# A graph network's issue order: seeds for a greedy planner, one per short stretch, in place of a small search

## The chip, the cores and the metric

The kernel runs on one core of one Trainium2 chip. The core has five engines that work side by side, each through its own queue and in order: PE (matrix multiply; PEld is its weight load, which overlaps the multiplies), DVE (vector), ACT (activation functions), POOL (general, slower than DVE) and SP, which here only issues DMA transfers. The metric is the time on the device in microseconds, from first to last instruction, and lower is better.

## The reference, cut to what matters

The input x holds 64 graphs of 256 nodes with 128 features, and one adjacency matrix of 256 x 256 serves all of them. Four layers follow one another, each closed by x = layernorm(x + layer(x)):

```python
for _ in range(5):                                     # layer 0: a gated recurrent graph network
    m = adj @ h
    u3 = h @ u3_w.T + u3_b
    z = sigmoid([m, m] @ w3_w.T + w3_b + u3)
    r = sigmoid([m, m] @ w4_w.T + w4_b + u3)
    hv = tanh([m, m] @ w5_w.T + w5_b + (r * h) @ u5_w.T + u5_b)
    h = (1 - z) * h + z * hv
y1 = (A * I) @ (x @ W[0]) + (A * (1 - I)) @ (x @ W[1]) + bias   # layer 1, A a softmax over edges
g  = relu(layernorm((softmax(scores) * adj) @ (x @ Wp + bp)))   # layer 2: attention, then an MLP
y2 = relu(relu(layernorm(((1 + eps) * g + adj @ g) @ W1 + b1)) @ W2 + b2 + g)
y3 = x @ V0 + sum_k (adj^k @ x) @ Vk                   # layer 3: powers 1 to 3, two sets of weights
```

Everything is in 32-bit floats. The graphs don't depend on one another.

## The kernel before, in words

The graphs are taken in 32 pairs. A tile of 128 partitions by 512 elements holds a pair: two graphs, two halves of the nodes, 128 features. One pair passes through the layers in a long chain of dependent steps, so many pairs are in flight together, and the order in which their steps stand in each engine's queue decides how well the engines are filled.

**The list of operations.** The code first records every step, without issuing it: `Schedule.add` takes the ways in which a step can be done (an engine, an expected duration in us, a function that issues it), what it reads and what it writes. `pe`, `act`, `dve`, `pool`, `evacuate`, `sum_` and `load` are short forms of it. Several steps have two or three ways, such as a sum by DVE or by POOL, or a copy out of PSUM by ACT or by DVE. A name "DVE+" is a DVE operation that uses the SBUF port which POOL uses too, so the planner lets it and a POOL operation exclude each other (`USES`, "PORT").

**The planner.** `order` places the operations one at a time. Of those whose predecessors are placed it takes the one with the smallest key (planned start, due time, number). The planned start is the latest of: its predecessors' ends with the latency to be seen and a lag of 0.3 us, a free buffer of each class it needs, and the free engine. Durations outside PE are multiplied by 1.1 (`MARGIN`). The due time (`op.late`) is 15 us per pair (12 for the last twelve), less the length of the rest of the pair's chain, with an offset for its layer. The result is one list, and the engines' queues are filled in its order. Buffers are given out by the planner too: 15 tiles for x (class X), 4 for the transposed input (T), 8 PSUM banks (PS), and so on.

**The search in it.** `run` goes ahead for 60 us of planned time (`WINDOW`) from a state (`Track`). From each state that was kept, 8 continuations are tried (`TRIES`). The first has no seed, the others add to the due time a pseudo-random number of up to 2 us (`NUDGE`), which depends on the operation's number and the seed. `place` keeps a second clock beside the planned one, with durations without margin and short latencies (`SOON`). It gives a "real" idle time of PE. The 4 states with the least idle time by both clocks (`KEPT`, `IDLE`) go on to the next window.

**The steps that the change touches.**
- `load_x` and `load_h` (by way of `load`, L348) bring a pair's input from DRAM, 256 KB each. The planner's three DMA numbers are the wait before the transfer, the transfer, and the time until its end is seen.
- `spread` (L636 on) multiplies adj with a pair: four matmuls of 256 columns. `spread7` (L647 on) does the same with seven matmuls of 128 columns and six sums on DVE or POOL, and one more copy out of PSUM. `FIRST` says from which pair on layer 0 uses `spread7`; before it, `spread` followed by `to_sbuf`.
- `scale_stats` and `scale_tokens` normalise (sums of squares, then a scaling), by ACT, DVE or POOL. `polynomial7` computes layer 3 with four sums of 256 columns.
- `turn` transposes a tile by a DVE transpose of 32x32 blocks, a write to DRAM and four reads back (L623, L625, L631). Every such DMA, every load and every store stands in SP's queue.

Of the kernel before, what the change touches and what calls it, by code (L numbers as in the profile page):

```python
# [24 lines left out]
FIRST, FINAL = 2, 0  # L25
# [33 lines left out]
SOON = {"PE": 0.2, "ACT": 0.17, "DVE": 0.15, "POOL": 0.15, "SP": 0.0}  # L59

WINDOW, TRIES, KEPT, NUDGE, IDLE = 60.0, 8, 4, 2.0, 0.3
# [45 lines left out]
class Schedule:  # L107
# [29 lines left out]
    def prepare(self, tiles):  # L137

        for op in self.ops:
            for b in op.before:  # L140
                b.then.append(op)
        for op in reversed(self.ops):
            us = min(w[1] for w in op.ways) + op.seen
            op.rest = us + max((x.rest for x in op.then if x.pair == op.pair), default=0.0)
        values = {}
        for op in self.ops:
            op.base = op.ways[0][0].rstrip("+-")
            op.late = self.due(op.pair) - op.rest + HOLD[op.layer] if op.pair >= 0 else -1e4
            op.plans = [(w[0], w[1] * (1.0 if w[0] == "PE" else MARGIN), w[1], USES.get(w[0], (w[0],)), SPARE.get(w[0], 0.0), k)
                        for k, w in enumerate(op.ways)]  # L150
            op.slots = []
            for v in op.holds:
                if v.cls:
                    if v not in values:
                        v.left, values[v] = 0, len(values)
                    v.left += 1
                    op.slots.append((values[v], v.cls, v.seeded, v.full or v.seeded))
        self.values = list(values)
        t = Track()
        t.waits = [len(op.before) for op in self.ops]  # L160
        t.since = [0.0] * len(self.ops)
        t.left, t.until, t.home = [v.left for v in values], [0.0] * len(values), [None] * len(values)
        t.free = {cls: [(0.0, k) for k in range(len(ts))] for cls, ts in tiles.items()}
        t.full = frozenset()
        t.engines, t.real = (dict.fromkeys([*SEEN, "PORT"], 0.0) for _ in range(2))
        t.ready, t.trail, t.number = [op for op in self.ops if not op.before], None, 0
        t.moved = t.real_moved = t.idle = t.real_idle = t.end = 0.0
        t.ends, t.owner, t.released = [0.0] * len(self.ops), {}, {}
        return t

    def run(self, t, until, seed):

        ready, engines, real = t.ready, t.engines, t.real
        while ready:
            best, homes = None, {}
            for op in ready:
                held = t.since[op.number]
                for v, cls, seeded, _ in op.slots:
                    if t.home[v] is None:
                        h = homes.get((cls, seeded))  # L180
                        if h is None:
                            h = homes[cls, seeded] = min((s for s, k in t.free[cls] if not seeded or (cls, k) in t.full),
                                                         default=1e9)
                        held = max(held, h)
                if held == 1e9:
                    continue
                way = None
                for engine, us, _, uses, spare, k in op.plans:
                    start = held
                    for e in uses:  # L190
                        start = max(start, engines[e])
                    if way is None or start + us + spare < way[0]:
                        way = start + us + spare, start, k
                late = op.late
                if seed and op.pair >= 0:
                    late += NUDGE * ((op.number * 7919 + seed * 104729) * 2654435761 % 4294967296 / 2147483648.0 - 1.0)
                key = (way[1], late, op.number)
                if best is None or key < best[0]:
                    best = key, op, way[2]
            if best is None:  # L200
                t.idle = t.real_idle = 1e9
                return
            (start, _, _), op, k = best
            if start >= until:
                return
            self.place(t, op, k, start)

    def place(self, t, op, k, start):

        engine, us, real_us, uses, _, _ = op.plans[k]  # L210
        base, engines, real = engine.rstrip("+-"), t.engines, t.real
        t.ready.remove(op)
        began = max(real[e] for e in uses)
        idle = began
        for x in op.before:
            later = 0.0 if x.base == base == "PE" else 0.05 if x.base == base != "SP" else SOON[x.base]
            began = max(began, t.ends[x.number] + later)
        for v, cls, seeded, full in op.slots:
            if t.home[v] is None:
                slot = min((s for s in t.free[cls] if not seeded or (cls, s[1]) in t.full), key=lambda s: s[0])  # L220
                t.free[cls].remove(slot)
                t.home[v] = slot[1]
                t.owner[v] = t.released.get((cls, slot[1]), 0.0)
            began = max(began, t.owner[v])
        if base == "PE":
            t.idle += start - engines["PE"]
            t.real_idle += began - idle
        end, real_end = start + us, began + real_us
        for e in uses:
            engines[e], real[e] = end, real_end  # L230
        seen, done = SEEN[base] + LAG, real_end + SOON[base]
        if op.dma:
            wait, move, after = op.dma
            t.moved = max(t.moved, end + wait) + move * MARGIN
            t.real_moved = max(t.real_moved, real_end + wait) + move
            seen, done = t.moved + after - end + LAG, t.real_moved + after
        t.ends[op.number] = done - SOON[base]
        t.end = max(t.end, done)
        t.trail, t.number = (t.trail, start, op, k), t.number + 1
        for v, cls, seeded, full in op.slots:  # L240
            home = cls, t.home[v]
            t.released[home] = max(t.released.get(home, 0.0), done)
            t.left[v] -= 1
            t.until[v] = max(t.until[v], end + seen)
            if not t.left[v]:
                t.free[cls].append((t.until[v], t.home[v]))
                t.full = t.full | {home} if full else t.full - {home}
        for x in op.then:
            t.waits[x.number] -= 1
            same = engine != "SP" and x.base == base  # L250
            t.since[x.number] = max(t.since[x.number], end + (AGAIN.get(base, 0.0) if same else seen))
            if not t.waits[x.number]:
                t.ready.append(x)

    def order(self, tiles):

        tracks, until, seed = [self.prepare(tiles)], 0.0, 0
        while any(t.ready for t in tracks):
            until += WINDOW
            found = []  # L260
            for t in tracks:
                for k in range(TRIES if t.ready else 1):
                    c = t.copy()
                    seed += 1
                    self.run(c, until, seed * bool(k))
                    found.append(c)
            tracks = sorted(found, key=lambda t: t.real_idle + IDLE * t.idle)[:KEPT]
        best = min((t for t in tracks if t.number == len(self.ops)), key=lambda t: t.end)
        self.span, self.best = max(best.engines.values()), best
        for v, k in zip(self.values, best.home):  # L270
            v.ap = tiles[v.cls][k]
        out, trail = [], best.trail
        while trail:
            trail, start, op, k = trail
            out.append((start, op.number, op, op.ways[k][2]))
        return [(op, fn) for _, _, op, fn in sorted(out, key=lambda x: x[:2])]


class Track:


    def copy(self):
        c = Track()
        for k, v in self.__dict__.items():
            setattr(c, k, dict(v) if type(v) is dict else list(v) if type(v) is list else v)
        c.free = {cls: list(s) for cls, s in self.free.items()}
        return c
# [3 lines left out]
def kernel(ctx: ExitStack, tc: tile.TileContext, x, xT, adj, adjT, mats, cols, rows, out):  # L291
# [65 lines left out]
    def load_h(p):  # L357
        load(lambda: hTs[p].at(2, N), xT[2 * p:2 * p + 2].rearrange("b d n -> d b n"), hTs[p])
# [720 lines left out]
```

## Time and profile before

| | |
|---|---|
| time, median of 3 runs | 1486.96 us (1486.75 to 1487.11) |
| profiled execution | 1486.49 us, span 1484.7 us |
| PE busy | 1468.3 us (99%) |
| DVE busy | 1270.5 us (86%) |
| ACT busy | 1044.6 us (70%) |
| POOL busy | 899.5 us (61%) |
| DMA | 216.65 MB, queue q1 at 71.4% of 16 engines |
| mean granted PE clock | 0.998 |

The span runs from the first to the last instruction. Busy time is the time in which an engine had an instruction running; the ends of matmuls are modelled, so a PE that is busy throughout isn't one at its peak. In lines of the profile, "L660 PE MATMUL ps<-aT,x" is line 660, on PE, writing a PSUM tile (ps) from the tiles aT and x. One matmul in 32-bit floats stands as two records. "[2.47 <-DMA x<-x_in]" means that the engine stood idle for 2.47 us ahead of this and that the load of x from its input was what it waited for. A view cut into stretches gives the busy time of each engine in each, with the clock that PE was granted (1.00 is full) and the busy share of the DMA engines.

### The profile page before, as it was taken

The numbers are of one execution on the slowest core, as the hardware profiler recorded it, in microseconds if no ns is written. First come the engines' busy times: TensorE is split into PE (matmuls) and PEld (weight loads), VectorE is DVE, ScalarE is ACT, GpSimd is POOL, SyncE is SP. The second block draws the span as 40 slices with busy tenths as digits, with TensorE's granted clock in tenths as the row PEclk, the third lists the DMA queues.
The fourth block names the chain that finished last, engine by engine and source line by source line (L and its number), as shares of the span: only waits on it lengthen the run. The fifth ranks groups of instructions, "written<-read, shape, count | busy, mean of one in ns | idle before, by whom it ended". The sixth has DMA issues, their size and how long they took to land.

```text
span 1484.7 us, 28833 instructions
## 1 busy us (share of the span) xinstructions
PE 1468.3 (99%) x8064; PEld 1066.6 (72%) x8064; DVE 1270.5 (86%) x3182; ACT 1044.6 (70%) x3185; POOL 899.5 (61%) x1383
## 2 busy tenths in 40 slices
PE   9999999999999999999999999999999999999997
PEld 6556666666677677777677777777777776788986
DVE  7867978989899899988889888888988879899973
ACT  4444566667788777776778786777777668789875
POOL 4322445465677687767755666556766656679752
PEclk9999999999999999999999999999999999999999
DMA  8544556778788887788787687767888766768662
GB/s 239 121 86 102 107 119 122 149 154 151 151 167 164 169 172 146 160 165 169 143 156 148 148 163 154 149 149 138 161 164 165 151 146 115 144 146 147 136 129 71
DMA packets 946848, 216.65 MB, mean 146 GB/s; under 512 B 726016, under 2 KB 942208, under 8 KB 946688
## 3 DMA queue, kind: packets, MB, share of 16 engines
q1 hardware_dynamic: 946688, 214.81, 71.4%
q8 instruction: 65, 1.06, 0.3%
q14 instruction: 95, 0.78, 0.2%
HBM read 116.86 MB, written 97.85 MB: 145 GB/s over the span
## 4 chain that ended last, share of the span: by engine, by line
PE 92%; DVE 5%; DMA 1%; ACT 1%; issue 1%; SPq 0%; POOL 0%; POOLq 0%; ACTq 0%; DVEq 0%
PE ps L660 23%; PE ps L778 9%; PE ps L779 9%; PE ps L786 9%; PE ps L793 9%; PE ps L794 9%; PE ps L815 7%; PE ps L994 5%; PE ps L915 4%; PE ps L1017 3%; PE ps L642 2%; PE ps L875 2%; DMA x<-x_in 1%; DVE a L623 0%; DVE x L711 0%
## 5 line engine op out<-in xcount | busy, mean ns | idle before, releaser
L660 PEld LDWEIGHTS ps<-aT,a 128*128 128x128 f32 x2144 | 290.2, 192 | 76.7 <-issue 66.5
L324 ACT COPY a<-ps 128x512 f32<-128x512 f32 (+2 forms) x588 | 243.0, 433 | 112.7 <-PE ps L660 41.3
L660 PE MATMUL ps<-aT,a 128*128 128x128 f32 x2144 | 315.8, 275 | 0.6 <-POOL a L666 0.6
L797 ACT ACTIVATE ps<-ps,bzrh 128x512 f32<-128x512 f32 x160 | 105.8, 661 | 108.7 <-PE ps L794 107.1
L782 ACT ACTIVATE a<-ps,bzrh 128x512 f32<-128x512 f32 x160 | 110.1, 688 | 102.1 <-PE ps L779 99.6
L739 ACT ACTIVATE a<-ps 128x128 f32<-128x128 f32 x496 | 130.9, 285 | 53.6 <-PE ps L815 20.4
L779 PE MATMUL ps<-a,w 128*128 128x512 f32 x320 | 164.3, 595 | 0.0
L793 PE MATMUL ps<-a,w 128*128 128x512 f32 x320 | 163.7, 593 | 0.5 <-DVE a L761 0.5
L679 POOL TENSOR_TENSOR a<-a 128x128 f32<-128x128 f32 x202 | 101.8, 508 | 103.0 <-DVE a L675 91.8
L794 PE MATMUL ps<-a,u5h 128*128 128x512 f32 x320 | 163.4, 592 | 0.0
L786 PE MATMUL ps<-a,w 128*128 128x512 f32 x320 | 163.4, 594 | 0.0
L623 DVE STREAM_TRANSPOSE a<-a 128x512 f32<-128x512 f32 x215 | 149.6, 698 | 2.4 <-ACT ps L324 0.4
L681 DVE TENSOR_TENSOR a<-ps,a 128x256 f32<-128x256 f32 x234 | 96.3, 415 | 60.0 <-ACT a L324 32.5
L815 PEld LDWEIGHTS ps<-W,a 128*128 128x128 f32 x1024 | 131.4, 192 | 15.7 <-issue 13.6
L815 PE MATMUL ps<-W,a 128*128 128x128 f32 x1024 | 142.7, 275 | 0.0
L747 POOL TENSOR_TENSOR s<-s,neg_half 128x4 f32<-128x4 f32 x128 | 138.2, 1080 | 6.9
L788 ACT ACTIVATE a<-ps,bzrh 128x512 f32<-128x512 f32 x160 | 110.6, 691 | 42.8 <-PE ps L786 39.0
L675 POOL TENSOR_TENSOR a<-a 128x256 f32<-128x256 f32 x114 | 84.9, 746 | 88.2 <-ACT a L324 85.9
L778 PE MATMUL ps<-a,W 128*128 128x512 f32 x256 | 131.6, 596 | 0.0
L779 PEld LDWEIGHTS ps<-a,w 128*128 128x128 f32 x320 | 61.1, 191 | 77.0 <-issue 68.2
L799 DVE SCALAR_TENSOR_TENSOR ps<-a,ps 128x512 f32<-128x512 f32 x160 | 109.3, 683 | 7.9 <-ACT a L788 6.4
L794 PEld LDWEIGHTS ps<-a,u5h 128*128 128x128 f32 x320 | 60.8, 190 | 76.5 <-issue 64.3
(229 smaller groups left out, 3454.9 us busy)
## 6 DMA issues: line engine op xcount, KB each, us to landing
e<-a SPq DMA_DIRECT2D x277, 256.0 KB
a<-e SPq DMA_DIRECT2D x1108, 64.0 KB
e<-b SPq DMA_DIRECT2D x32, 512.0 KB
b<-e SPq DMA_DIRECT2D x128, 128.0 KB
x<-x_in SPq DMA_DIRECT2D x32, 256.0 KB
t<-xT_in SPq DMA_DIRECT2D x32, 256.0 KB
a<-d SPq DMA_DIRECT2D x32, 256.0 KB
y_out<-a SPq DMA_DIRECT2D x32, 256.0 KB
```

What stands on the lines that cost most here:

```text
L324: S.add([("ACT", us[0], lambda: nc.scalar.copy(o(), i())), ("DVE", us[1], lambda: nc.vector.tensor_copy(o(), i()))], r, w)
L623: dve(n / 512 * 0.55 + 0.09, lambda: nc.vector.transpose(st.at(n), i.at(n)), [i], [st])
L660: pe(mm(128), lambda: nc.tensor.matmul(blk(t, k), left(), rt(), start=start, stop=True, skip_group_check=True), [*r, right, terms, *[t] * ...
L739: nc.scalar.activation(tokens(junk)[:, c, :], v.at(len(tiles), D)[:, k, :], AF.Square, scale=D ** -0.5, accum_out=mv()[:, c, 1:2])
L747: pool(1.02, lambda: nc.gpsimd.tensor_tensor(rs(), rs(), neg_half.ap, op=ALU.pow), [s, neg_half], [s])
L778: nc.tensor.matmul(t.at(512), mat("u3"), hT.at(512), start=True, stop=False)
L779: nc.tensor.matmul(t.at(512), w4.ap, mT.at(512), start=False, stop=True)
L786: pe(mm(512), lambda t=t, mT=mT: nc.tensor.matmul(t.at(512), w3.ap, mT.at(512), start=False, stop=True, skip_group_check=True), [w3, mT, t ...
L788: act(0.59, lambda t=t, z=z: nc.scalar.activation(z.at(512), t.at(512), AF.Tanh, bias=bzrh.ap[:, 0:1], scale=0.5), [t, bzrh], [z])
L793: nc.tensor.matmul(t.at(512), w5.ap, mT.at(512), start=True, stop=False)
L794: nc.tensor.matmul(t.at(512), u5h.ap, r.at(512), start=False, stop=True)
L815: nc.tensor.matmul(tokens(t)[:, c, :], tokens(i)[:, c, :], w(), start=(first and k == c == 0), stop=(k == len(lefts) - 1), skip_group_chec ...
```

## The change

The change concerns the planner and its prices. The operations, their inputs and their results stay, but for one shape (`FIRST`).

- The search leaves the kernel: `run`, `place`, `Track` and the second clock are gone. `order` is now a single greedy pass with the same key. Each 15 us of planned time have a seed from a list of 99 numbers, `SEEDS`, of which 30 aren't zero. A seed other than zero adds to the due time a pseudo-random number of up to 1, 2 or 3 us (by the seed's remainder by 3), from a better mixed hash (`shuffled`). The list was found ahead of time, outside the kernel.
- A candidate that can start only later than the best so far is left out early, which doesn't change the choice.
- The planner's DMA numbers for loads change: for x from (0.6, 1.04, 0.9) to (0.6, 1.33, 2.5), for the transposed input from (0.6, 1.04, 0.9) to (0.6, 1.05, 1.5).
- The planner's durations change for POOL sums (0.8 to 0.69, 0.46 to 0.42, 1.27 to 1.235) and for the ACT ways of normalising (0.285 and 0.315 to 0.255 per token tile).
- `FIRST` goes from 2 to 1: pair 1 uses `spread7` in its five steps of layer 0.

```diff
-FIRST, FINAL = 2, 0
+FIRST, FINAL = 1, 0
-SOON = {"PE": 0.2, "ACT": 0.17, "DVE": 0.15, "POOL": 0.15, "SP": 0.0}
-
-WINDOW, TRIES, KEPT, NUDGE, IDLE = 60.0, 8, 4, 2.0, 0.3
+WINDOW, NUDGE = 15.0, 1.0
+
+XLOAD, TLOAD = (0.6, 1.33, 2.5), (0.6, 1.05, 1.5)
+
+SEEDS = [0, 113, 0, 0, 0, 0, 0, 0, 0, 0, 0, 0, 0, 0, 0, 0, 0, 0, 0, 0, 0, 0, 0, 0, 0, 0, 0, 0, 99747, 109039, 0,
+         127395, 136626, 145860, 0, 172027, 0, 0, 192033, 202672, 213506, 0, 0, 0, 0, 0, 0, 0, 0, 0, 0, 0, 0, 0,
+         0, 0, 0, 0, 0, 0, 0, 0, 0, 0, 431775, 441535, 451905, 0, 0, 0, 0, 0, 0, 516963, 526274, 0, 544854, 0, 0,
+         0, 585026, 0, 0, 0, 622370, 631520, 639000, 646717, 658660, 667211, 0, 681297, 690347, 700377, 708021,
+         726295, 727034, 736340, 0]
...
-    def run(self, t, until, seed):
-    def place(self, t, op, k, start):
...
+            best, homes, seed = None, {}, SEEDS[window] if window < len(SEEDS) else 0
             for op in ready:
...
                 late = op.late
                 if seed and op.pair >= 0:
-                    late += NUDGE * ((op.number * 7919 + seed * 104729) * 2654435761 % 4294967296 / 2147483648.0 - 1.0)
+                    late += NUDGE * (1 + seed % 3) * shuffled(op.number, seed)
                 key = (way[1], late, op.number)
...
+            (start, _, _), op, (_, _, engine, us, uses, fn) = best
+            if start >= (window + 1) * WINDOW:
+                window += 1
+                continue
...
-        load(lambda: xs[p].at(4, D), x[2 * p:2 * p + 2].rearrange("b (t p) d -> p (b t) d", p=P), xs[p])
+        load(lambda: xs[p].at(4, D), x[2 * p:2 * p + 2].rearrange("b (t p) d -> p (b t) d", p=P), xs[p], dma=XLOAD)
...
-        sum_(0.335, 0.8, lambda e: e.tensor_sub(sv.at(4, P)[:, 0:2], h.at(4, P)[:, 0::2], h.at(4, P)[:, 2:4]), [h], [p1])
-        sum_(0.2, 0.46, lambda e: e.tensor_sub(s2(), s1(), H(0, 0)()), [h, p1], [p2])
+        sum_(0.335, 0.69, lambda e: e.tensor_sub(sv.at(4, P)[:, 0:2], h.at(4, P)[:, 0::2], h.at(4, P)[:, 2:4]), [h], [p1])
+        sum_(0.2, 0.42, lambda e: e.tensor_sub(s2(), s1(), H(0, 0)()), [h, p1], [p2])
...
-            S.add([("ACT", 0.285 * n, by_act), ("DVE", 0.267 * n, by_dve)], [v], [st, s, junk])
+            S.add([("ACT", 0.255 * n, by_act), ("DVE", 0.267 * n, by_dve)], [v], [st, s, junk])
...
-        ways = [("ACT", 0.315 * n, by_act),
+        ways = [("ACT", 0.255 * n, by_act),
```

More of the change, by code (lines that the diff above doesn't have):

```diff
@@ L135, in due, with prepare @@
         return DUE * (pair - late) + LAST_DUE * late
-    def prepare(self, tiles):
+    def prepare(self):
         for op in self.ops:
@@ L144, in prepare @@
             op.rest = us + max((x.rest for x in op.then if x.pair == op.pair), default=0.0)
-        values = {}
         for op in self.ops:
@@ L148, in prepare @@
             op.late = self.due(op.pair) - op.rest + HOLD[op.layer] if op.pair >= 0 else -1e4
-            op.plans = [(w[0], w[1] * (1.0 if w[0] == "PE" else MARGIN), w[1], USES.get(w[0], (w[0],)), SPARE.get(w[0], 0.0), k)
-                        for k, w in enumerate(op.ways)]
-            op.slots = []
+            op.plans = [(w[0], w[1] * (1.0 if w[0] == "PE" else MARGIN), USES.get(w[0], (w[0],)), SPARE.get(w[0], 0.0), w[2])
+                        for w in op.ways]
+            op.holds = [v for v in op.holds if v.cls]
@@ L152, in prepare @@
+            op.waits, op.since = len(op.before), 0.0
             for v in op.holds:
[L153 to L169, printed above, removed]
-    def run(self, t, until, seed):
-        ready, engines, real = t.ready, t.engines, t.real
+                v.left, v.end, v.home = v.left + 1, 0.0, None
@@ L174, in run, with order, slots @@
+    def order(self, tiles):
+        self.prepare()
+        engines = dict.fromkeys([*SEEN, "PORT"], 0.0)
+        free = {cls: [(0.0, k) for k in range(len(ts))] for cls, ts in tiles.items()}
+        ready, full, moved, out, window = [op for op in self.ops if not op.before], set(), 0.0, [], 0
+        def slots(v):
+            return [s for s in free[v.cls] if not v.seeded or (v.cls, s[1]) in full]
         while ready:
-            best, homes = None, {}
+            best, homes, seed = None, {}, SEEDS[window] if window < len(SEEDS) else 0
@@ L176, in run @@
             for op in ready:
[L177 to L184, printed above, removed]
@@ L185, in run @@
-                if held == 1e9:
+                held = op.since
+                for v in op.holds:
+                    if v.home is None:
+                        if (v.cls, v.seeded) not in homes:
+                            homes[v.cls, v.seeded] = min((s for s, _ in slots(v)), default=1e9)
+                        held = max(held, homes[v.cls, v.seeded])
+                if held == 1e9 or best and held > best[0][0]:
                     continue
                 way = None
[L188 to L191, printed above, removed]
+                for engine, us, uses, spare, fn in op.plans:
+                    start = max(held, *(engines[e] for e in uses))
@@ L192, in run @@
                     if way is None or start + us + spare < way[0]:
-                        way = start + us + spare, start, k
+                        way = start + us + spare, start, engine, us, uses, fn
                 late = op.late
                 if seed and op.pair >= 0:
-                    late += NUDGE * ((op.number * 7919 + seed * 104729) * 2654435761 % 4294967296 / 2147483648.0 - 1.0)
+                    late += NUDGE * (1 + seed % 3) * shuffled(op.number, seed)
                 key = (way[1], late, op.number)
@@ L198, in run @@
                 if best is None or key < best[0]:
-                    best = key, op, way[2]
+                    best = key, op, way
             if best is None:
[L201 to L206, printed above, removed]
-    def place(self, t, op, k, start):
[L210 to L275, printed above, removed]
-        return [(op, fn) for _, _, op, fn in sorted(out, key=lambda x: x[:2])]
@@ L279 @@
[L279 to L287, printed above, removed]
+                raise RuntimeError("the shared tiles are too few for this order")
+            (start, _, _), op, (_, _, engine, us, uses, fn) = best
+            if start >= (window + 1) * WINDOW:
+                window += 1
+                continue
@@ new lines, in order @@
+            ready.remove(op)
+            for v in op.holds:
+                if v.home is None:
+                    slot = min(slots(v), key=lambda s: s[0])
+                    free[v.cls].remove(slot)
+                    v.home, v.ap = slot[1], tiles[v.cls][slot[1]]
+            end, base = start + us, engine.rstrip("+-")
+            for e in uses:
+                engines[e] = end
+            seen = SEEN[base] + LAG
+            if op.dma:
+                wait, move, after = op.dma
+                moved = max(moved, end + wait) + move * MARGIN
+                seen = moved + after - end + LAG
@@ new lines, in order @@
+            out.append((start, op.number, op, fn))
+            for v in op.holds:
+                v.left, v.end = v.left - 1, max(v.end, end + seen)
+                if not v.left:
+                    free[v.cls].append((v.end, v.home))
+                    (full.add if v.full or v.seeded else full.discard)((v.cls, v.home))
+            for x in op.then:
+                same = engine != "SP" and x.base == base
+                x.waits, x.since = x.waits - 1, max(x.since, end + (AGAIN.get(base, 0.0) if same else seen))
+                if not x.waits:
+                    ready.append(x)
@@ L290, with shuffled @@
+        self.span = max(engines.values())
+        return [(op, fn) for _, _, op, fn in sorted(out, key=lambda x: x[:2])]
+def shuffled(number, seed):
+    x = number * 2654435761 & 0xFFFFFFFF ^ seed * 2246822519 & 0xFFFFFFFF
+    x = (x ^ x >> 15) * 2246822519 & 0xFFFFFFFF
+    x = (x ^ x >> 13) * 3266489917 & 0xFFFFFFFF
+    return (x ^ x >> 16) / 2147483648.0 - 1.0
 @with_exitstack
@@ L318, in dve_or_pool @@
     def dve_or_pool(fn, r, w):
-        S.add([("DVE+", TT, lambda: fn(nc.vector)), ("POOL", 1.27, lambda: fn(nc.gpsimd))], r, w)
+        S.add([("DVE+", TT, lambda: fn(nc.vector)), ("POOL", 1.235, lambda: fn(nc.gpsimd))], r, w)
     def evacuate(o, i, r, w, us=(0.49, 0.61)):
@@ L346, in row, with load @@
         return rbc.ap[:, None, i * D:(i + 1) * D].to_broadcast([P, n, D])
-    def load(o, i, v, kb=256):
-        S.add([("SP", 0.45, lambda: nc.sync.dma_start(o(), i))], [], [v], (0.6, kb / 245, 0.9))
+    def load(o, i, v, kb=256, dma=None):
+        S.add([("SP", 0.45, lambda: nc.sync.dma_start(o(), i))], [], [v], dma or (0.6, kb / 245, 0.9))
     xs = [Value("X", name=f"x{p}") for p in range(n_pairs)]
@@ L354, in load_x @@
     def load_x(p):
-        load(lambda: xs[p].at(4, D), x[2 * p:2 * p + 2].rearrange("b (t p) d -> p (b t) d", p=P), xs[p])
+        load(lambda: xs[p].at(4, D), x[2 * p:2 * p + 2].rearrange("b (t p) d -> p (b t) d", p=P), xs[p], dma=XLOAD)
     def load_h(p):
-        load(lambda: hTs[p].at(2, N), xT[2 * p:2 * p + 2].rearrange("b d n -> d b n"), hTs[p])
+        load(lambda: hTs[p].at(2, N), xT[2 * p:2 * p + 2].rearrange("b d n -> d b n"), hTs[p], dma=TLOAD)
     pool(1.0, lambda: nc.gpsimd.iota(diff.ap, pattern=[[1, P]], base=0, channel_multiplier=-1,
@@ L664, in sum_ @@
             S.add([("DVE+", us, lambda: fn(nc.vector)), ("POOL", us_pool, lambda: fn(nc.gpsimd))], r, w)
-        sum_(0.335, 0.8, lambda e: e.tensor_sub(sv.at(4, P)[:, 0:2], h.at(4, P)[:, 0::2], h.at(4, P)[:, 2:4]), [h], [p1])
-        sum_(0.2, 0.46, lambda e: e.tensor_sub(s2(), s1(), H(0, 0)()), [h, p1], [p2])
-        sum_(0.2, 0.46, lambda e: e.tensor_add(s4(), s2(), H(0, 1)()), [h, p2], [p4])
+        sum_(0.335, 0.69, lambda e: e.tensor_sub(sv.at(4, P)[:, 0:2], h.at(4, P)[:, 0::2], h.at(4, P)[:, 2:4]), [h], [p1])
+        sum_(0.2, 0.42, lambda e: e.tensor_sub(s2(), s1(), H(0, 0)()), [h, p1], [p2])
+        sum_(0.2, 0.42, lambda e: e.tensor_add(s4(), s2(), H(0, 1)()), [h, p2], [p4])
         product(0, H(0, 0), B(0, 0), [h], start=True)
@@ L674, in spread7 @@
         evacuate(lambda: o.at(512), lambda: t.at(512), [t], [o])
-        sum_(0.335, 0.8, lambda e: e.tensor_add(sv.at(4, P)[:, 0:2], o.at(4, P)[:, 0:2], o.at(4, P)[:, 2:4]), [o], [p1])
+        sum_(0.335, 0.69, lambda e: e.tensor_add(sv.at(4, P)[:, 0:2], o.at(4, P)[:, 0:2], o.at(4, P)[:, 2:4]), [o], [p1])
         product(0, H(0, 1), B(1, 0), [h])
@@ L678, in spread7 @@
         product(1, s4, B(1, 1), [p4])
-        sum_(0.2, 0.46, lambda e: e.tensor_add(blk(o, 3), blk(sv, 0), blk(sv, 1)), [p1], [o])
+        sum_(0.2, 0.42, lambda e: e.tensor_add(blk(o, 3), blk(sv, 0), blk(sv, 1)), [p1], [o])
         evacuate(lambda: blk(o, 0), lambda: blk(t, 0), [t], [o], (0.17, 0.2))
@@ L859, in layer1 @@
         S.add([("ACT", 1.26, scaled), ("DVE+", TT, lambda: nc.vector.tensor_mul(xd.at(2, 2, D), x1.at(2, 2, D), dc())),
-               ("POOL", 1.27, lambda: nc.gpsimd.tensor_mul(xd.at(2, 2, D), x1.at(2, 2, D), dc()))], [x1, dcol], [xd])
+               ("POOL", 1.235, lambda: nc.gpsimd.tensor_mul(xd.at(2, 2, D), x1.at(2, 2, D), dc()))], [x1, dcol], [xd])
         dT = turn(xd, "dT", "x1")
@@ L982, in sum_ @@
             S.add([("DVE+", us, lambda: fn(nc.vector)), ("POOL", us_pool, lambda: fn(nc.gpsimd))], r, w)
-        sum_(0.335, 0.8, lambda e: e.tensor_sub(S3(), x0(), x1()), [xT], [s3])
-        sum_(0.335, 0.8, lambda e: e.tensor_sub(S2(), q1(), S3()), [qT, s3], [s2])
-        sum_(0.335, 0.8, lambda e: e.tensor_add(S1(), x1(), q1()), [xT, qT], [s1])
-        sum_(0.335, 0.8, lambda e: e.tensor_sub(S4(), q0(), S2()), [qT, s2], [s4])
+        sum_(0.335, 0.69, lambda e: e.tensor_sub(S3(), x0(), x1()), [xT], [s3])
+        sum_(0.335, 0.69, lambda e: e.tensor_sub(S2(), q1(), S3()), [qT, s3], [s2])
+        sum_(0.335, 0.69, lambda e: e.tensor_add(S1(), x1(), q1()), [xT, qT], [s1])
+        sum_(0.335, 0.69, lambda e: e.tensor_sub(S4(), q0(), S2()), [qT, s2], [s4])
         y, t = bank(), Value("PS", name="ps")
```

## The prediction

> **What bounds the kernel now.** I read the page first, then the busy table cut into stretches of 15 us, then PE's waits, then the order of time around the largest of them.
>
> ```profile
> span 1484.7 us, 28833 instructions
> PE 1468.3 (99%) x8064; PEld 1066.6 (72%) x8064; DVE 1270.5 (86%) x3182; ACT 1044.6 (70%) x3185; POOL 899.5 (61%) x1383
> ```
>
> PE (matrix multiply) has work in all but 1484.7 − 1468.3 = 16.4 us. The change removes almost no matmul, so what it can win is in these 16.4 us, and in matmuls that ran slowly. The stretches say where they lie (columns: stretch, length, then busy time and count of PE, PEld, DVE, ACT, POOL, granted clock, DMA share, GB/s):
>
> ```profile
> 480.00:495.00 15.00, 15.00 (x96) 11.65 (x96) 14.30 (x41) 11.88 (x42) 11.07 (x17) 1.00 0.97 195
> 495.00:510.00 15.00, 12.13 (x46) 6.69 (x45) 10.55 (x30) 9.65 (x27) 8.24 (x14) 0.89 0.86 170
> 525.00:540.00 15.00, 14.47 (x78) 9.97 (x77) 13.41 (x42) 12.26 (x40) 11.84 (x18) 1.00 0.96 162
> 1350.00:1365.00 15.00, 14.74 (x100) 12.71 (x99) 14.96 (x45) 13.05 (x46) 14.23 (x19) 1.00 0.71 132
> 1365.00:1380.00 15.00, 14.39 (x112) 13.73 (x111) 14.97 (x47) 14.31 (x64) 14.67 (x22) 1.00 0.69 147
> 1410.00:1425.00 15.00, 13.17 (x97) 12.04 (x96) 14.38 (x45) 13.21 (x57) 8.56 (x15) 1.00 0.84 170
> 1455.00:1470.00 15.00, 13.55 (x79) 12.15 (x78) 7.53 (x25) 9.10 (x34) 4.92 (x8) 1.00 0.37 90
> 1470.00:1485.00 15.00, 8.13 (x36) 6.20 (x34) 1.27 (x3) 4.99 (x23) 2.52 (x4) 0.94 0.29 69
> ```
>
> Nearly every stretch not shown has PE at 15.00. The holes are: 1.2 us at the start; 2.87 + 0.53 us in two stretches of the middle; 0.40 + 0.26 + 0.61 + 0.50 + 0.11 + 1.83 + 1.45 = 5.2 us between 1335 and 1470; and 6.9 us in the last 15. The largest hole, in order of time, PE alone, then its releaser in the list of waits, then the chain there:
>
> ```profile
> 497.66 1.13 PE L778 MATMUL ps<-t,W 128*128 128x512 f32 x2 [0.40 <-DVE a L681]
> 499.70 1.02 PE L786 MATMUL ps<-a,w 128*128 128x512 f32 x2
> 503.20 0.46 PE L660 MATMUL ps<-aT,x 128*128 128x128 f32 x2 [2.47 <-DMA x<-x_in]
> 503.50 1.70 PE L778 MATMUL ps<-a,W 128*128 128x512 f32 x2
> ...
> PE ps L660 <- DMA x<-x_in: 2.5, 1, 2.5
> PE ps L1017 <- DVE a L1013: 1.9, 2, 1.5
> ...
> 498.57 4.50 DMA x<-x_in
> 503.06 0.14 issue
> 503.20 0.46 PE ps L660 x2
> 503.66 1.54 PE ps L778 x2
> 505.20 1.71 PE ps L779 x2
> ```
>
> The reader is to see three things. An input load issued at 498.57 is seen only 4.50 us later, and the whole PE queue stands behind the matmul that reads it. After it the L778 pair takes 1.54 us instead of 0.86 (the same pair elsewhere), because the clock fell: 0.89 over 15 us is 15 × 0.11 = 1.65 us lost. This one event so costs 0.40 + 2.47 + 1.65 = 4.5 us. And from 1335 on the holes are of another kind: DVE is full (14.96 and 14.97 of 15), few pairs are left, and PE waits for DVE results.
>
> **What the skill says.** "TensorE: Matmul & The Clock Gate", section "What's actually happening", says that the array's clock falls to half after an idle window of about 3.4 us and returns after a busy one. The trace agrees on half speed and on the way back; the gap itself was 2.47 us, with 0.40 us shortly before, so here less than a full idle window sufficed. "SBUF — State Buffer", section "SBUF: two separate sides", says that a DVE operation with two SBUF inputs and a POOL operation lock each other out for a whole instruction. The trace agrees in kind: the DVE form of L666 on x has a median of 414 ns and a longest of 1495. The planner models this as PORT, before and after. "DMA: Bandwidth & Descriptors", section "Latency and other measured facts", gives an HBM access 0.2 us on average and 2 us at high load; the 4.50 us load fell where the DMA share was 0.86 to 0.97.
>
> **The change part by part.** No operation changes what it computes; their order, their engines where there is a choice, and one small shape change.
>
> 1. *The price of a load of x.* Before, the planner takes 0.6 + 256/245 + 0.9 = 2.5 us after the issue; the trace shows 4.50 − 0.43 (issue) = 4.1. After, 0.6 + 1.33 + 2.5 = 4.4. The old plan put the reader about 2 us too early, which is most of the 2.47 us. With the new price another matmul is placed ahead, if one is ready. The hole and its slow clock, 4.5 us, can go; the 0.53 us one at 530 (a DVE wait in a stretch whose DMA share is 0.96) is for the seeds. Together −5.0.
>
> 2. *Seeds.* Before: 60 us windows, 8 tries, 4 tracks kept, durations partly wrong. After: 99 windows of 15 us, 30 with a seed, the others plain greedy. The values run to 736340, so many orders stand behind each. A seed only decides between operations that could start at the same planned time; in a queue with work waiting that is the usual case. The seeded windows lie (in planned time) at 15, within 420 to 615, 960 to 1155, at 1200 and within 1260 to 1470 us, thickest where the trace has its holes, which suggests that the search saw the same ones. It can move DVE work forward out of the full stretch at 1350 (DVE has 1.7 to 4.2 us free in each stretch from 1155 to 1245). I take 3.0 of the 5.2 us as won; the bounds are 0 (DVE full, nothing moves) and 5.2.
>
> 3. *Prices of POOL and ACT.* POOL sums go from 0.8 to 0.69 (× 1.1 = 0.76; traced 0.746 for L675, 0.766 to 0.786 for L666), and 0.46 to 0.42 (× 1.1 = 0.46; traced 0.49 to 0.53). ACT squares 0.285 to 0.255 each (traced start to start 0.25). More sums go to POOL (61% busy) and more normalising to ACT (70%), away from DVE (86%): good in the tail, with POOL's 128x128 sums under-priced by some 0.05 us. I count it inside part 2.
>
> 4. *FIRST from 2 to 1.* Pair 1 forms its five layer-0 products in seven blocks. The plain form takes 1.73 us (4 matmuls of 256 columns), the seven take 7 × 0.223 = 1.56 (eight take 1.78 in the chain). 5 × 0.17 = −0.85 us of PE. Added: five times six DVE or POOL sums (0.43 + 0.28 + 0.29 + 0.43 + 0.35 + 0.41 = 2.2 us), 11 us in all, and 5 × 0.27 on ACT. From 60 to 135 us DVE is busy 8 to 11 of 15, which hides them; from 15 to 45 it is busy 13.5 and 14.5, and the first one sits at 6.5 to 8.3, where its plain matmuls fill PE while the weights arrive. Bounds −0.85 and +2; I take −0.3.
>
> 5. *New holes.* A new order has its own misses: I allow two of the 0.5 us kind, +1.0. The last stretch stays: after the final matmul come square, power, scale and store, some 6 us, which no order shortens.
>
> 6. *DMAs.* The same number; SP issues all of them in order, so each moved turn moves its five issues past others (a load or store, at 0.45 us each). Bounded by the rivals below.
>
> Sum: −5.0 − 3.0 − 0.3 + 1.0 = −7.3, so the span becomes 1477.4. The runs' median is 1486.96 − 1484.7 = 2.26 us above the profiled span: 1479.6 us.
>
> **Rivals.**
> - *The tail doesn't move* (DVE is the bound there, 14.97 of 15, and POOL at 14.67 has no room): −4.3, 1482.7. For it: three engines are near full at 1365. Against: ACT and POOL have 3.7 and 5 us free at 1380 to 1395.
> - *All goes right*: −5.0 − 5.2 − 0.85 and no new hole, −11, 1475.9. Against: holes in the last pairs come from one chain with nothing beside it.
> - *The stall moves.* One late transfer finds PE without other work elsewhere: −7.3 + 4.5 = −2.8, 1484.2, no measurable change. For it: one DMA queue at 71% of 16 engines, and DMA shares of 0.9 to 1.05 in many stretches.
> - *Slower: late transfers under a tight order.* The search fitted one set of durations; every turned tile passes SP and the DMA twice, and in SP's waits L631 stands 176.1 us for the first half to land. If the new order places readers close behind, each miss costs PE a hole, and at about 2.5 us the half clock as well, 4.5 us. Two cancel the gain (−7.3 + 9 = +1.7), three make it +6.2, 1493.2. Against: the order itself is still chosen with durations × 1.1 and 0.3 us of lag, and the old order with that slack had only one such miss.
> - *It does nothing*: seeds that never meet a tie would leave plain greedy. Part 1 would still act; counted with the first rival.
>
> **How the numbers follow.** Forecast 0.50, tail stays 0.19, all right 0.08, stall moves 0.11, slower 0.12. A measurement here can't tell less than 0.2%, 3.0 us, from no change. Faster: 0.50 + 0.19 + 0.08 = 0.77; same 0.11; slower 0.12. The range: below, the best case and a little (1475); above, the moved stall and a hole more (1487); outside it lie the slower case and part of the best, under 2 in 10. The likeliest case alone: 1476.5 to 1482, from the bounds of parts 2 and 4.
>
> **What would show it.** Part 1: no PE wait on x_in over 1 us, and clock 1.00 in every stretch until 1470. Part 2: PE's holes from 1335 to 1470 sum to 2 to 3 us, with DVE below 14.9 at 1350 to 1380. Part 3: a larger POOL busy sum than 899.5 and a smaller DVE than 1270.5. Part 4: the plain product with aT (L642) drops from 112 to 72 matmul records, and no PE hole before 60. A half-clock stretch in the middle would make the forecast wrong, as would a PE hole behind a turned tile.

## The result and the profile after

The changed kernel takes 1477.53 us (median of 4 runs, 1476.44 to 1479.21), against 1486.86 us before: a ratio of 0.9941, 95% interval 0.9923 to 0.9958. Run again later beside others, it took 1477.35 us, ratio 0.9934 (0.9921 to 0.9947). The profiled span fell from 1484.7 to 1475.4 us. The page's head:

```profile
span 1475.4 us, 28934 instructions
PE 1463.8 (99%) x8094; PEld 1065.6 (72%) x8094; DVE 1265.9 (86%) x3123; ACT 1052.5 (71%) x3246; POOL 931.5 (63%) x1440
```

The idle time of PE fell from 16.4 to 11.6 us, its busy time by 4.5 us. The stretches that answer to those of before, same columns:

```profile
495.00:510.00 15.00, 14.85 (x87) 10.70 (x86) 13.17 (x39) 13.89 (x52) 12.20 (x19) 1.00 0.85 177
525.00:540.00 15.00, 15.00 (x99) 12.36 (x99) 13.78 (x47) 12.41 (x43) 10.45 (x18) 1.00 0.76 159
1350.00:1365.00 15.00, 15.00 (x124) 14.66 (x124) 14.61 (x53) 14.07 (x59) 13.47 (x20) 1.00 0.82 164
1365.00:1380.00 15.00, 15.00 (x114) 14.38 (x113) 14.55 (x40) 14.12 (x54) 12.30 (x17) 1.00 0.64 131
1410.00:1425.00 15.00, 14.50 (x106) 13.57 (x105) 12.97 (x39) 12.16 (x56) 10.55 (x16) 1.00 0.89 167
1455.00:1470.00 15.00, 13.69 (x63) 11.39 (x61) 1.20 (x3) 8.42 (x40) 2.96 (x6) 1.00 0.40 96
```

The hole of 2.87 us at 495 is down to 0.15 us and the clock is 1.00; 1350 to 1380 has no hole; what is missing from 15.00 in the last line is the end of PE's work at 1468.7. PE's waits after, all of them that are listed:

```profile
PE ps L330 <- DVE ones L328: 1.2, 1, 1.2
PE ps L606 <- DVE a L880: 0.9, 1, 0.9
PE ps L606 <- DVE a L612: 0.6, 2, 0.5
PE ps L732 <- ACT a L728: 0.6, 1, 0.6
PE ps L861 <- issue: 0.5, 1, 0.5
PE ps L861 <- DMA b<-e: 0.5, 1, 0.5
PE ps L940 <- DVE a L957: 0.3, 1, 0.3
PE ps L606 <- DMA a<-e: 0.2, 1, 0.2
```

No input load is among them, and none is over 1.2 us. Two are for turned tiles (b<-e and a<-e, 0.5 and 0.2 us).

**A finer ruler.** The busy table hides short gaps, since records overlap, and counts half-clock matmuls as work. So I take, from the starts of the matmul records, each record's distance to the next less the median distance of its shape (112 ns for 128 columns, 216 for 256, 429 for 512), and sum it. I call it PE's lost time. Before it is 16.3 us, after 7.0 us; the sum of the medians falls by 0.8 us (the smaller work of pair 1), and the last matmul's start to the end of the span grows by 0.78 us. −9.3 − 0.8 + 0.8 gives the 9.3 us of the span. By stretch, for one profiled execution of every kernel that ran (the values are good to some 0.3 us, as the medians are rounded, and a small negative one says no more than that):

| kernel | time, us | 0 to 20 | 20 to 420 | 420 to 600 | 600 to 1335 | 1335 to end |
|---|---|---|---|---|---|---|
| before | 1486.9 | 2.1 | 0.0 | 5.7 | −0.3 | 8.8 |
| before, another execution (e12) | 1485.7 | 2.2 | 0.5 | 3.4 | −0.5 | 9.9 |
| changed | 1477.5 | 3.1 | −0.3 | 0.9 | 0.8 | 2.6 |
| changed, again (e9) | 1477.4 | 4.0 | −0.3 | 1.1 | −0.1 | 2.0 |
| e1: no seeds | 1489.9 | 3.2 | 1.4 | 3.0 | 2.1 | 9.5 |
| e2: no seeds from 1260 | 1489.6 | 3.2 | −0.5 | 1.1 | 2.5 | 16.2 |
| e11: no seeds from 1365 | 1481.7 | 3.3 | −0.3 | 1.1 | 0.7 | 6.0 |
| e6: other seeds from 1260 | 1487.3 | 3.6 | −0.2 | 1.7 | 1.3 | 10.8 |
| e7: FIRST 2, same seeds | 1499.0 | 2.8 | 0.6 | 3.3 | 4.3 | 18.2 |
| e3: before, one product moved | 1484.8 | 2.8 | −0.2 | 3.0 | −0.4 | 8.2 |
| e4: before, load prices | 1482.3 | 2.9 | −0.5 | 1.9 | 0.1 | 6.0 |
| e5: before, all prices | 1482.4 | 2.7 | −0.3 | 0.1 | 2.8 | 6.3 |
| e8: all prices, wider search | 1490.8 | 2.0 | −0.3 | 1.5 | 2.2 | 12.5 |
| e10: changed, two moves | 1476.2 | 3.0 | −0.3 | 1.8 | 0.7 | 2.2 |

### The profile page after: what moved, and what is told of

Its sections match the earlier page's. It is cut to its first block, busy times and chain, and to the rows that moved or that the text cites. A ratio compares the mean times of both kernels' runs of the same rounds, so it can differ in the third digit from the quotient of the medians.

```text
span 1475.4 us, 28934 instructions
## 1 busy us (share of the span) xinstructions
PE 1463.8 (99%) x8094; PEld 1065.6 (72%) x8094; DVE 1265.9 (86%) x3123; ACT 1052.5 (71%) x3246; POOL 931.5 (63%) x1440
## 4 chain that ended last, share of the span: by engine, by line
PE 95%; DVE 2%; DMA 1%; ACT 1%; SPq 0%; issue 0%; POOLq 0%; ACTq 0%; POOL 0%; DVEq 0%
PE ps L606 24%; PE ps L732 9%; PE ps L739 9%; PE ps L740 9%; PE ps L724 9%; PE ps L725 9%; PE ps L761 7%; PE ps L940 6%; PE ps L861 4%; PE ps L963 4%; PE ps L588 2%; PE ps L821 2%; DMA a<-e 0%; SPq L577 0%; PE ps L563 0%
## 5 line engine op out<-in xcount | busy, mean ns | idle before, releaser
L606 PEld LDWEIGHTS ps<-aT,a 128*128 128x128 f32 x2208 | 301.9, 192 | 81.6 <-issue 73.5
L270 ACT COPY a<-ps 128x512 f32<-128x512 f32 (+2 forms) x590 | 246.1, 433 | 127.4 <-PE ps L606 58.1
L606 PE MATMUL ps<-aT,a 128*128 128x128 f32 x2208 | 330.6, 275 | 0.7 <-DVE a L612 0.5
L685 ACT ACTIVATE a<-ps 128x128 f32<-128x128 f32 x508 | 134.2, 285 | 44.3 <-PE ps L761 19.4
L627 DVE TENSOR_TENSOR a<-ps,a 128x256 f32<-128x256 f32 x239 | 99.5, 418 | 74.4 <-ACT a L270 37.6
L621 POOL TENSOR_TENSOR a<-a 128x256 f32<-128x256 f32 x125 | 93.5, 751 | 100.5 <-ACT a L270 95.8
```

Source lines behind the costliest of these rows:

```text
L270: S.add([("ACT", us[0], lambda: nc.scalar.copy(o(), i())), ("DVE", us[1], lambda: nc.vector.tensor_copy(o(), i()))], r, w)
L606: pe(mm(128), lambda: nc.tensor.matmul(blk(t, k), left(), rt(), start=start, stop=True, skip_group_check=True), [*r, right, terms, *[t] * ...
L685: nc.scalar.activation(tokens(junk)[:, c, :], v.at(len(tiles), D)[:, k, :], AF.Square, scale=D ** -0.5, accum_out=mv()[:, c, 1:2])
```

## The experiments

**Are the seeds needed, or do prices and greedy do?** e1 sets all seeds to zero, e2 those from window 84 on, e11 those from 91 on. The planner goes forward only, so in e2 and e11 the order is that of the changed kernel up to the first zeroed window.

```diff
-         0, 585026, 0, 0, 0, 622370, 631520, 639000, 646717, 658660, 667211, 0, 681297, 690347, 700377, 708021,
-         726295, 727034, 736340, 0]
+         0, 585026, 0, 0, 0, 0, 0, 0, 0, 0, 0, 0, 0, 0, 0, 0,
+         0, 0, 0, 0]
```

> The changed kernel with all 99 seeds zero: the plain greedy order at the new prices, pair 1 in seven products. Theory (the seeds carry the gain, the prices alone don't): PE's holes of the old kind come back in the middle and in the tail, 1484 to 1495 us, at least 6 us above the changed kernel's 1477.5. Rival (the mended prices and the freed search are enough, seeds are decoration): 1476 to 1480 us.

> The changed kernel with the seeds of the windows from 84 on (planned time 1260 us) set to zero. The planner is causal, so the order is the same up to there. Theory (the tail's holes are a matter of order, and its seeds win some 4 us): PE's holes after 1335 us grow from 1.7 us to 5 or 6 us, the holes before stay as they are, 1481 to 1484 us. Rival (the tail is bound by DVE's sum of work, which the seeds don't change): 1477 to 1479 us, holes after 1335 under 3 us.

Measured: e1 1489.92 us, ratio to before 1.0024 (1.0014 to 1.0034): without seeds the change would be a loss. e2 1489.58 us, 1.0026 (1.0015 to 1.0037): taking only the tail's seeds away costs 12 us, more than I expected of it by far. PE's waits in its profile from 1335 us on, the longest (the profiled execution, 1492.1 us, is the slowest of its eight):

```profile
PE ps L587 <- ACT a L704: 4.0, 1, 4.0
PE ps L587 <- DVE a L869: 1.3, 1, 1.3
PE ps L939 <- ACT a L269: 1.0, 1, 1.0
```

One wait of 4.0 us for a normalising on ACT stands in the stretch from 1365, which has PE at 11.23 of 15 and a clock of 0.97; at 1380 the clock is 0.81. The rival (a tail set by DVE's sum of work) falls: the operations are the same, DVE is busy 107.7 us from 1335 on against 102.8, and the lost time there goes from 2.6 to 16.2 us. Some 5 us of this are two stretches at half clock, of 6.8 and 3.4 us.

> The changed kernel with seeds up to window 90 and none from planned 1365 us on. Theory (the tail's gain is spread over its windows): half of the 12 us that came back without any seed from 1260 on, 1482 to 1486 us, holes only after 1365 us. Rival (the stretch where DVE is full, 1335 to 1365, is what had to be got right): within 2 us of the changed kernel.

Measured: 1481.66 us, ratio 0.9962 (0.9951 to 0.9974), 4.3 us above the changed kernel beside it. The tail's gain is spread over its windows: some 8 of the 12 us come from the seeds between 1260 and 1365, 4 from those after (by the ratios, each to its own runs of before, 9.5 of 13.7 and 4.2).

**These draws or any?** e6 raises each seed from window 84 on by 3, which keeps the amplitude of its shuffle.

> The changed kernel with each of the 13 seeds from window 84 on raised by 3: the same amplitude of shuffle, another draw; the order is the same up to 1260 us of planned time. Theory (what counts is that these draws were picked out of thousands): holes of 8 to 15 us after 1335 us as without tail seeds, 1484 to 1492 us. Rival (any shuffle breaks the bad ties): 1477 to 1480 us.

Measured: 1487.27 us, ratio 1.0002 (0.9993 to 1.0012). This other draw is worth 2 to 4 us over none (by medians or by ratios, as the two were timed beside different runs of before) and 9 to 10 us less than the one in the list. Its longest wait in the tail is one that the changed kernel hasn't, for a turned tile:

```profile
PE ps L903 <- DMA a<-e: 2.9, 1, 2.9
```

**Do the seeds stand for themselves?** e7 undoes one part, FIRST, and keeps each operation's number, so that the shuffles stay.

```diff
-FIRST, FINAL = 1, 0
+FIRST, FINAL = 2, 0
...
+            S.skip += 12 * (S.pair == 1)
```

> The changed kernel with FIRST back at 2 (pair 1 in plain products), every later operation keeping its number, so that each seed shuffles the same operations in the same way. Theory (the seeds fit one course of the plan; a start that differs by under 1 us puts them out of tune): holes in the middle and the tail as without seeds, 1486 to 1494 us, though the hole at 7 us is gone and PE has 0.8 us more to do. Rival (the seeds name orders that are good in themselves): 1477 to 1480 us.

Measured: 1498.95 us, ratio 1.0071 (1.0057 to 1.0084), 7 to 9 us worse than no seeds at all. One shape in one pair, 0.8 us of PE work and the sums that go with it, is enough to make the list harmful. It says nothing of FIRST by itself; that is read from the profiles, below.

**How much is the price of the loads?** e4 gives the kernel before the new DMA prices alone; e5 also those of POOL and ACT. Both run the old search anew.

```diff
-    def load(o, i, v, kb=256):
-        S.add([("SP", 0.45, lambda: nc.sync.dma_start(o(), i))], [], [v], (0.6, kb / 245, 0.9))
+    def load(o, i, v, kb=256, dma=None):
+        S.add([("SP", 0.45, lambda: nc.sync.dma_start(o(), i))], [], [v], dma or (0.6, kb / 245, 0.9))
...
-        load(lambda: xs[p].at(4, D), x[2 * p:2 * p + 2].rearrange("b (t p) d -> p (b t) d", p=P), xs[p])
+        load(lambda: xs[p].at(4, D), x[2 * p:2 * p + 2].rearrange("b (t p) d -> p (b t) d", p=P), xs[p], dma=(0.6, 1.33, 2.5))
```

> The kernel before with only the new DMA prices of its input loads (for x 0.6, 1.33, 2.5; for the transposed input 0.6, 1.05, 1.5); its own search runs anew. Theory (the price of the load made the stall): no PE wait on an x load over 0.5 us and no half clock in the middle; the tail keeps holes of 4 to 6 us, 1481 to 1484 us. Rival (the stall was an accident of one order, the prices don't matter): a new order with other holes, no systematic loss of the wait on x, 1485 to 1490 us.

> The kernel before with all new prices (loads, POOL sums, ACT normalising), its own search run anew, FIRST still 2. Theory (the POOL and ACT prices add something to the load prices, as they take work off DVE): POOL busy over 920 us, fewer tail holes than with the load prices alone, 1478 to 1481 us. Rival (beyond the loads only the seeds count): like the load prices alone, 1481 to 1484 us.

Measured: e4 1482.25 us, ratio 0.9977 (0.9967 to 0.9986); e5 1482.41 us, 0.9967 (0.9955 to 0.9980), beside its own runs of before. Both orders are some 3.5 us faster than before, with no PE wait on x listed; the intervals overlap, so of the POOL and ACT prices no gain of their own is shown, though POOL does take more (924.7 us busy). In neither did the middle alone shrink: both tails lose 6 us in place of 9. A changed price gives a new order everywhere, so it isn't shown that the price and not the redraw won the 3.5 us: two redrawn orders agree, but the old search was not redrawn at the old prices, and e8 below is a slower order at the new ones.

**The stall by itself.** e3 keeps the old order but for one matmul (two records): the first product on x16 goes behind five PE steps.

```diff
-        for op, fn in S.order(tiles):
+        order = S.order(tiles)
+        k = next(i for i, (op, _) in enumerate(order) if op.base == "PE" and xs[16] in op.reads)
+        j = next(i for i, (op, _) in enumerate(order) if op.base == "PE" and op in order[k][0].then)
+        order.insert(j - 1, order.pop(k))
+        for op, fn in order:
```

> The kernel before, with one matmul pair moved: the first product that reads x16, which stood 2.47 us for its load, goes behind five other PE steps of some 4 us, to just ahead of the next product of its own bank. Theory (the stall and the half clock after it cost what they show): the 2.47 us hole and the 1.71 us lost to the half clock go, the time falls by 3.5 to 4.5 us to some 1483 us, clock 1.00 in all stretches of the middle. Rival (PE's time there is taken from a later wait: what is saved is lost again at the next hole): less than 1.5 us of gain, with the holes at 530 us or in the tail grown by as much.

> The kernel before, unchanged, profiled in another execution. Theory (the stall on x16 belongs to the order): a PE wait on x_in of 2 to 3 us at 503 us and the half clock again; then the small gain from moving the product away means that the time was given back at later waits. Rival (the stall belongs to that one execution: the load landed late by chance): no wait on x over 1 us and a clock of 1.00 there; then the moved product could win little because there was mostly nothing to win.

Measured: e3 1484.77 us, ratio 0.9993 (0.9987 to 0.9999), a gain of 1.1 us and not of 4. First, the half clock isn't in every execution of the kernel before. Of the 40 timed beside e3, 17 have a mean granted clock of 0.998, as the first profile has, and take 1487.1 us in the mean; the other 23, at 0.999 or 1.000, take 1485.1. Of the 21 of e3 two have 0.998, and the other 19 take 1484.9 in the mean. So what e3 wins is mostly that the lower clock becomes rare. Where it fell in the executions without a profile isn't recorded. Second, the kernel before itself, profiled again in e12 (mean clock 0.999), has a smaller hole at that place and no half clock:

```profile
495.00:510.00 15.00, 13.03 (x58) 7.79 (x57) 11.89 (x33) 12.16 (x33) 9.93 (x14) 1.00 0.90 179
...
502.88 0.25 ACT L324 COPY a<-ps 128x128 f32<-128x128 f32 x1
503.01 0.81 POOL L666 TENSOR_TENSOR a<-x 128x256 f32<-128x256 f32 x1 [2.48 <-DMA x<-x_in]
503.05 0.30 PEld L660 LDWEIGHTS ps<-aT,x 128*128 128x128 f32 x2 [2.42 <-ACT b L902]
503.08 0.46 PE L660 MATMUL ps<-aT,x 128*128 128x128 f32 x2 [1.62 <-ACT b L902]
```

Here the profile names ACT, and in the first profile it names ACT on the weight load too:

```profile
503.13 0.73 POOL L666 TENSOR_TENSOR a<-x 128x256 f32<-128x256 f32 x1 [3.32 <-DMA x<-x_in]
503.17 0.30 PEld L660 LDWEIGHTS ps<-aT,x 128*128 128x128 f32 x2 [3.27 <-ACT b L902]
```

That name is no second cause. The weight load waits for the load of x and for a point in ACT's queue, and the profile names the signal that came last. In both executions PE goes 0.04 us after the POOL sum that waits for the same load of x, and in e12 it starts at 503.08, before ACT's copy out of PSUM ends at 503.13. So both holes fit the load alone, and that ACT held the matmul up is not shown. In e12 the POOL sum starts 3.84 us after the load's issue, in the first profile 4.56. My expectation's theory and rival were both half right for e12: a hole belongs to this place, but its size and the half clock change from one execution to the next.

Third, in e3's profile PE has a longer wait at 528 us:

```profile
PE ps L793 <- DVE a L761: 1.4, 1, 1.4
```

It was 0.53 us in the first profile, and e12 lists none there; the chain behind it is the load of a row of scores (a<-d, 5.50 us) that DVE's queue stands for. So some of the gain may be lost again here, but with one profile of e3 this isn't shown.

**Is it the width of the search?** e8 is e5 with windows of 100 us, 32 tries and 8 kept.

> The kernel before with all new prices and a wider search of its own (windows of 100 us, 32 tries, 8 kept, in place of 60, 8 and 4). Theory (how wide the search is decides, wherever it runs): 1475 to 1479 us, level with the changed kernel. Rival (the short windows with a seed each are what matters, or the second clock is too rough for a wider search to use): like the same prices with the small search, within 1.5 us of it.

Measured: 1490.82 us, ratio 1.0024 (1.0016 to 1.0032), 8 us worse than the small search. Both orders were picked by the same second clock; more candidates to pick from didn't help. (Window, tries and kept states changed together, so this says nothing of each alone.) PE's longest waits there:

```profile
PE ps L915 <- DMA b<-e: 3.4, 2, 2.1
PE ps L957 <- DMA a<-e: 1.6, 1, 1.6
PE ps L660 <- DMA a<-e: 1.2, 1, 1.2
```

All three are for turned tiles. That the second clock rates such tiles too favourably, so that a wider search finds the orders that profit from it, would fit this, but it wasn't tried.

**A version beyond the change.** In the profile after, two losses looked like single instructions out of place. e10 moves both; e9 is the changed kernel beside it.

```diff
-            scale_tokens(t, o, range(i, 4, 2), s, rs)
+            scale_tokens(t, o, range(i, 4, 2), s, rs, by_dve=(i == 1 and p == n_pairs - 1))
...
+        k = next(i for i, (op, _) in enumerate(order) if op.base == "DVE" and op.reads == [xs[1]])
+        j = next(i for i, (op, _) in enumerate(order) if w4 in op.writes)
+        order.insert(j, order.pop(k))
```

> The changed kernel once more, as the base of the two that run beside it: 1476 to 1479.5 us. If the hole structure is the order's own, PE's excess after 1335 us stays under 4 us in this execution too; if it was luck of one profile, it will be nearer the 6 to 9 us of the old orders.

> The changed kernel with two single instructions placed otherwise. At the end, the last pair's second half is scaled by DVE, which is idle, beside ACT, where the new ACT price had put both halves on ACT one after the other: 0.5 us less from the last matmul to the end. At the start, the DVE sum of x1 stands ahead of the sum of two weights that waits for its load: the 0.45 us PE hole at 7 us goes. Theory (both are on the path that sets the end): 0.7 to 1.0 us under the changed kernel beside it, 0.05%, at the edge of what the rounds tell; the profile shows both. Rival (the start's hole only moves to the next wait, as the middle's did): only the 0.5 us of the end.

Measured: e9 1477.35 us; e10 1476.21 us, ratio to before 0.9930 (0.9918 to 0.9943), lower than e9 by 1.1 us in the medians, with intervals that overlap. The end, in order of time: first before, then after, then e10.

```profile
1480.93 0.42 DVE L761 TENSOR_TENSOR a<-ps,s 128x256 f32<-128x256 f32 x1 [5.95 <-POOL s L747]
1480.93 0.63 ACT L759 ACTIVATE a<-ps,s 128x128 f32<-128x128 f32 x2 [1.47 <-POOL s L747]
...
1470.84 1.14 ACT L705 ACTIVATE a<-ps,s 128x128 f32<-128x128 f32 x4 [1.45 <-POOL s L693]
...
1471.29 0.63 ACT L705 ACTIVATE a<-ps,s 128x128 f32<-128x128 f32 x2 [1.46 <-POOL s L693]
1471.29 0.42 DVE L707 TENSOR_TENSOR a<-ps,s 128x256 f32<-128x256 f32 x1 [9.72 <-POOL s L693]
```

The lower ACT price made the planner put both halves of the last scaling on ACT, one behind the other, while DVE had nothing to do: from the last matmul's start to the end 7.08 us (7.07 in e9), and 6.28 in e10 against 6.30 before. Of the 0.78 us more, 0.5 are the longer scaling; the rest follows it. The start hole, which was 0.45 us in the first profile and 1.21 us in e9, is down to 0.2 us in e10, with 0.16 us more for a load of the transposed input; the first weight matmul of layer 0 starts at 8.13 us there, at 8.29 and 9.21 in the two profiles of the changed kernel. The shorter end is shown; of the start only the worse of the two profiles is bettered, so the rival isn't excluded for it. And the spans of the two profiles, 1475.07 us in e10 and 1475.09 in e9, are the same: e10 loses as much between 420 and 1335 us, so a gain in the time itself isn't shown.

## Why the prediction was right, point by point

The forecast of 1479.6 us was 2.1 us high. That it came so near is partly luck, as two of its terms were off in opposite directions. The terms of its sum, measured by lost time between the two first profiles:

- *Part 1 and the stall, −5.0.* In these two profiles 420 to 600 us gives −4.8. But the term was read from one execution: the half clock and nearly 1 us of the hole aren't in e12, against which the middle gives −2.5. The load was rightly named as what PE waited for. Its old price was short by 4.1 − 2.5 = 1.6 us, not by about 2. For the new load prices speak e4 and e5 (e4: −3.6 us), each with one redrawn order; that they act through this one stall isn't borne out, since e4's tail shrinks as well.
- *Part 2, the tail, −3.0 with bounds 0 and 5.2.* This is the mis-sized term: 8.8 to 2.6, −6.2, and −7.9 from e12 to e9. The upper bound was too small because I summed the busy table, which shows 5.2 us of holes from 1335 to 1470 and hides part of every gap under the overlap of the records; 1.2 of the 8.8 us lie after 1470, where I had counted on no change. The picture of DVE work moved forward isn't borne out either. The first profile after has DVE at 14.61 at 1350, but e9, at the same time of its own order, reads

```profile
1350.00:1365.00 15.00, 15.00 (x124) 14.64 (x123) 14.94 (x54) 14.07 (x59) 13.50 (x20) 1.00 0.81 168
```

  A DVE just as full goes with a PE without a hole. What counts is which step stands first in the queue; why these orders do better, step by step, I can't say.
- *Part 3.* POOL 899.5 to 931.5 us, DVE 1270.5 to 1265.9: as foretold, and with no gain that e5 could show. That the ACT price would lengthen the very end I had missed (0.78 us, 0.5 of it from the scaling); I had written that no order shortens that stretch, and this one made it longer.
- *Part 4, FIRST, −0.3 with bounds −0.85 and +2.* The matmul work fell by 0.79 us, and the plain product with aT from 112 records to 72. The loss in the first 20 us is 2.0 to 2.9 us in the seven profiles with FIRST at 2 (before, e3, e4, e5, e7, e8, e12; mean 2.5), and 3.1 to 4.0 in the six with FIRST at 1 and nothing moved (after, e1, e2, e6, e9, e11; mean 3.4). So +0.9 − 0.8: no gain of this part is shown. "No PE hole before 60 us" was wrong: 0.45 and 1.21 us, behind the first DVE sum of pair 1.
- *Part 5, new holes, +1.0.* 600 to 1335 us: +1.1 in the first profile, +0.2 in e9.
- *The slower rival* didn't come about here, but its mechanism exists: e6 and e8 are slower orders with waits of up to 2.9 and 2.1 us for turned tiles, and e2 and e7 have the half clock too, though after waits for other things.
- *"It does nothing"* is out: the seeds are worth 12.4 us over plain greedy (e1).

So the forecast was near for a sum in which the middle was priced too high and the tail too low. Against e12 in place of the first profile, both errors are larger, and still of opposite sign. The marks set for it: no wait on x and a clock of 1.00 until 1470 came true; tail holes of 2 to 3 us were 1.7; DVE below 14.9 holds in one profile of two. Of the signs that would have spoken against it, the half clock in the middle didn't show; waits for turned tiles did, at 0.5 and 0.2 us.

## What to carry to other kernels

Before pricing a stall, look at it in more than one execution: taking away a stall that showed 2.5 us and a half clock gave 1.1 us. Where an instruction has several waits, look at who else waits for the same load, since the name beside a wait can be that of a bystander. Near the end of a pipeline, where few items are left, the order alone can be worth 12 us with the same work, and busy time doesn't show whether an order is good. A list of seeds fits one course of the plan, so that any later change of shape or price needs a new search (e7: some 20 us), and a wider search can end in a slower order (e8).

## What the runs showed that I had not expected

- A PE hole of 2.47 us was followed by 3.4 us at half clock (0.89 over the stretch), while one of 1.62 us in another execution of the same kernel left it at 1.00. But the length of the hole alone doesn't decide it: in e6 a hole of 2.92 us, at 1470 us, left the clock at 1.00 for the 5.7 us of matmuls after it, and in e7 one of 2.85 us, at 1385 us, was followed by 3.4 us at half clock.
- The load of x, 256 KB, takes from 3.3 to 5.5 us from issue to landing in the profile after, median 4.4: the spread is as wide as the error of the old price.
- Two executions of one order differ by 0.8 us in one short stretch (0.45 and 1.21 us of hole at 7 us), where a DVE instruction stands behind another that waits for a load.
